# Expert activations of a hybrid scan, attention and mixture kernel: the bias out of the bank first, Gelu in runs of four

## The chip, the cores and the metric

The kernel runs on one core of one Trainium2 chip, in float32. The metric is device time in microseconds (us) of one execution. TensorE multiplies matrices into PSUM banks; VectorE, ScalarE and GpSimd do elementwise work; SyncE (SP) issues nearly all the DMAs. Each engine runs its own queue of instructions strictly in order, and waits on semaphores where an operand comes from another engine.

## The reference, cut to what matters

The input is x of shape (4, 384, 32, 32). Layer 0 is a selective scan in four directions over each image, with 16 states a channel; layer 1 turns the image into 1024 tokens of 384 values per batch, and applies local attention and then a mixture of four experts, of which each token uses two.

```
# layer 0, for each of 4 directions, channel d and state n, over l = 1..1024
dt = softplus(W_dt @ x_dt + bias);  dA = exp(dt * A[d, n])
h[l] = h[l-1] * dA[l] + dt[l] * u[l] * B[n, l];   y[l] += h[l] * C[n, l]
x = x + gelu(layernorm(merge(y)) * lnw + lnb)           # exact gelu
# layer 1
t = t + attention(layernorm(t))                         # 6 heads, causal, window 64
h = gelu(layernorm(t) @ w1[e] + b1[e])                  # 384 -> 1536, exact gelu
t = t + sum over the 2 best experts e of p[e] * (h @ w2[e] + b2[e])
```

Two activation functions matter for what follows. Exp (and Ln) belongs to the decays dA, the time steps dt and the attention's softmax. Gelu belongs to the end of layer 0 and to the experts' first layer.

## The kernel before

**The parts.** Each piece of work is a Python generator. For layer 0: `time_steps` makes dt; `decay` (L830) makes dA = exp(dt * a) on ScalarE, one tile of 128x1024 for each of 768 slots; `times_b` makes z = dt*u*B on GpSimd; `scan` (L856) runs the recurrence on VectorE; `times_c` (L843) multiplies by C, on VectorE or on GpSimd; `fold_y` sums the states with matmuls into a bank ps_y. dA has two buffers of two PSUM banks each (`das_`), so that a decay can only be written when an earlier scan, or the multiplication by C after it, has let go of its buffer. z has seven buffers (`zs_`).

For layer 1: `tokens` (its `tile` is at L986) finishes layer 0 for 128 tokens, with three Gelus on a bank ps_g, and does the attention; `route` picks experts and scatters tokens into rows by expert; `loads` brings in a block of 128 rows and its expert's weights; `hidden` (L1388) is the first layer, `gelus` (L1409) its activation, `output` (L1420) the second layer; `combine` gathers the two results for each token. There are 76 blocks, 19 for each batch. A block's 1536 first-layer values are made in four chunks of 384, each in one PSUM bank ps_hid and then in one tile hs of 128x384, of which there are four. `output` takes a block up when all four of its hs tiles are there.

**What sets the order.** The order of each engine's queue is fixed when the program is built. A planner, `Machine`, keeps a clock per engine and a cost per instruction. Each generator yields its next instruction; `choose` (L338) takes for each engine the one that is ready first, with a bias (`GELU_BIAS`, `LATER` and others). On ScalarE it prefers what needs the activation tables that are loaded now, unless another has been ready for more than 3 us of the planner's time (`PATIENCE`). Where tables change, a table load stands ahead of the activation: the one back to Exp is written by hand (`load_exp_ln`, L304), the one to Gelu has the line of the helper that issues the activation (L148). `Calls` collects several instructions, and `all` (L150) hands them to the planner as one, so that nothing else comes between them. The planner's clocks also decide whether a `times_c` goes to VectorE or GpSimd, and whether copies and some biases go to VectorE or ScalarE. So a change in one place moves instructions everywhere.

**Shared buffers.** Four PSUM banks (`banks`) serve everything but dA: dt, the folds, all the token steps, both expert layers and the routing. When the last scan is done, the two dA buffers join them.

In the profile most instructions have line L148 or L159, the two helpers that issue them, and are told apart by their tiles.

Of the kernel before, what the change touches and what calls it, by code (L numbers as in the profile page):

```python
# [12 lines left out]
AF = mybir.ActivationFunctionType  # L13
# [4 lines left out]
P = 128  # L18
# [18 lines left out]
CH = 384  # L37
NCH, HT = HID // CH, CH // P
# [98 lines left out]
class Engine:  # L137
# [12 lines left out]
    def all(self, calls):  # L150

        asked = [self.ask(*c) for c in calls]
        outs, ins = ([ap for o in asked for ap in getattr(o, side)] for side in ("outs", "ins"))
        table = next((o.table for o in asked if o.table), None)
        whole = Op(self.name, outs, ins, sum(o.cost for o in asked), table, 0)
        whole.work = sum(o.work for o in asked)
        yield whole
        for op, a, k in calls:
            getattr(self.real, op)(*a, **k)  # L159
# [233 lines left out]
def conv_attn_hybrid(  # L393
# [98 lines left out]
    with tc.tile_pool(name="setup", bufs=1) as setup:  # L492
# [16 lines left out]
        for j in range(JB):  # L509
            ps = banks.now("ps_al")  # L510
# [61 lines left out]
    pe, act, dve, pool, sp = m.pe, m.act, m.dve, m.pool, m.sp  # L572
# [315 lines left out]
    ended = []  # L888
# [45 lines left out]
    def three(name, src):  # L934

        yield m.settled(src)
        ps = yield from banks.take(name)
        mm = Calls()
        for t in range(T):
            mm.transpose(ps[:, ts(t, P)], src[:, ts(t, P)], ident)  # L940
        yield from pe.all(mm)
        return ps
# [18 lines left out]
    def normal_of(dst, ps):  # L961
        rn = yield from norm(ps)
        yield from act.activation(dst[:, :D], ps[:, :D], AF.Identity, bias=rn[:, 1:2], scale=rn[:, :1])
        banks.give(ps)
        rns.give(rn)

    def tokens(b):
# [18 lines left out]
        def tile(a):  # L986
# [11 lines left out]
            ps = yield from three("ps_y0", w)  # L998
            yield from normal_of(w, ps)
            g = yield from three("ps_g", w)  # L1000
            for t in range(T):
                yield from act.activation(
                    g[:, ts(t, P)], g[:, ts(t, P)], AF.Gelu,
                    bias=lnb_sb[:, t : t + 1], scale=lnw_sb[:, t : t + 1],
                )
            yield from dve.tensor_tensor(tt[:, :D], g[:, :D], tt[:, :D], ALU.add)
            banks.give(g)
            ps = yield from three("ps_t", tt)
            yield from normal_of(w, ps)
            xt = yield from rows.take("xt")  # L1010
            ps = yield from three("ps_x1", w)
# [7 lines left out]
            for n, (w, dst) in enumerate(  # L1019
                ((wq, q[:, :D].rearrange("p (t l) -> p t l", t=T)), (wk, kv[:, :, :P]))  # L1020
            ):
                ps = yield from banks.take("ps_qk")
                mm = Calls()
# [7 lines left out]
                if not on_vector():  # L1031
                    for o in range(T):
                        yield from act.activation(
                            dst[:, o, :], ps[:, ts(o, P)], AF.Identity,
                            bias=qkb_sb[:, n * T + o : n * T + o + 1],
# [14 lines left out]
            ps = yield from banks.take("ps_v")  # L1050
            mm = Calls()
# [41 lines left out]
            for hp in range(T):  # L1093
                for j in range(2):
                    h = 2 * hp + j
# [29 lines left out]
            mm = Calls()  # L1125
# [22 lines left out]
            ps = yield from three("ps_ot", o)  # L1148
# [3 lines left out]
            ps = yield from banks.take("ps_pr")  # L1152
            on_act = not on_vector()
            mm = Calls()
# [10 lines left out]
            for o in range(T):  # L1165
                c = ts(o, P)
# [12 lines left out]
            ps = yield from three("ps_t2", tt)  # L1179
# [6 lines left out]
            ps = yield from three("ps_xt", tt)  # L1186
            rows.give(tt)
            yield from copy(xt[:, :D], ps[:, :D])
            mm = Calls()
# [8 lines left out]
            have.add(("token", b, a))  # L1198

        yield from m.together([tile(a) for a in range(NT)], TILES, EARLY)  # L1200
        wts.give(wq, wk, wv, wp)

# [156 lines left out]
    rws, bbs, xts, w1s, w2s, hids, left = {}, {}, {}, {}, {}, {}, {}  # L1359
# [28 lines left out]
    def hidden():  # L1388
        for i in range(len(ffn)):
            for c in range(NCH):  # L1390
                hs = yield from hss.take("hs")
                yield lambda: i in xts and (i, c) in w1s
                yield m.settled(xts[i], w1s[i, c])
                ps = yield from banks.take("ps_hid", HID_RANK)
                w = w1s.pop((i, c))
                mm = Calls()
                for j in range(HT):
                    for t in range(T):
                        mm.matmul(
                            ps[:, ts(j, P)], w[:, t * CH + j * P : t * CH + j * P + P],  # L1400
                            xts[i][:, ts(t, P)], start=t == 0, stop=t == T - 1,
                        )
                yield from pe.all(mm)
                wts.give(w)
                if c == NCH - 1:
                    xbts.give(xts.pop(i))
                m.spawn(gelus(i, c, ps, hs), GELU_BIAS)

    def gelus(i, c, ps, hs):  # L1409
        for j in range(HT):  # L1410
            jj = c * HT + j
            yield from act.activation(
                hs[:, ts(j, P)], ps[:, ts(j, P)], AF.Gelu, bias=bbs[i][:, jj : jj + 1]
            )
        banks.give(ps)
        hids[i, c] = hs
        if c == NCH - 1:
            bbs_.give(bbs.pop(i))

    def output():  # L1420
        for i in range(len(ffn)):
            for c in range(NCH):
                yield lambda: (i, c) in hids and (i, c) in w2s
            yield m.settled(*(hids[i, c] for c in range(NCH)))
            y = yield from banks.take("y_ff")
            for c in range(NCH):
                mm = Calls()
                for j in range(HT):
                    mm.matmul(
                        y[:, :D], hids[i, c][:, ts(j, P)], w2s[i, c][:, ts(j, D)],  # L1430
                        start=c == 0 and j == 0, stop=c == NCH - 1 and j == HT - 1,
                    )
                yield from pe.all(mm)
                wts.give(w2s.pop((i, c)))
                hss.give(hids.pop((i, c)))
            m.spawn(leave(i, y), LATER)
# [146 lines left out]
```

## Time and profile before

| | us |
|---|---|
| three runs | 3930.62, 3936.42, 3939.96 (median 3936.42) |
| the profiled execution: its time | 3933.02 |
| its span, first to last instruction | 3931.3 |

| engine | busy us | share of the span | instructions |
|---|---|---|---|
| PE (TensorE) | 3031.9 | 77% | 15880 |
| DVE (VectorE) | 2911.4 | 74% | 3331 |
| POOL (GpSimd) | 2879.7 | 73% | 1498 |
| ACT (ScalarE) | 2441.7 | 62% | 4050 |

The granted TensorE clock has a mean of 0.819 of full speed. DMA moved 953.66 MB, at a mean of 243 GB/s.

A group in the profile reads "line, engine, operation, output tile <- input tiles, shapes, xcount | busy us, mean ns of one | idle us of the engine just before them, and what ended most of it". A wait reads "engine, tile <- the engine and tile that ended the wait: us in total, times, longest us". The largest group of ScalarE is the decay, 768 of 128x1024 at 1116 ns; a scan takes VectorE 2276 to 2287 ns, and times_b takes GpSimd 2358 ns. A line of the timeline is "start us, us, engine, line, operation, xcount", with idle time before it in brackets.

### The profile page before, as it was taken

To read this page: it belongs to the slowest core of one execution; us is meant where nothing else is said; L and a number is where in the kernel's file an instruction comes from. 1 tells how busy PE (TensorE), PEld (TensorE's weight loads), DVE (VectorE), ACT (ScalarE), POOL (GpSimd) and SP (SyncE) were. 2 spreads that over 40 slices of the span, in tenths; PEclk is the share of its full clock that TensorE was granted. 3 is DMA by queue.
4 is the path that set the end of the run, shared out by engine and by line. 5 is a ranking of instruction groups with operands and counts; after the bars stand their busy time and mean duration, and the time that the engine had idled before them with its cause. 6 is when DMAs were issued, how large, how long until landed. Compare 5 with 4: busy or idle time off the path is not lost. (4 is left out here: it accounts for less than half of the span.)

```text
span 3931.3 us, 50281 instructions
## 1 busy us (share of the span) xinstructions
PE 3031.9 (77%) x15880; PEld 1853.6 (47%) x15880; DVE 2911.4 (74%) x3331; ACT 2441.7 (62%) x4050; POOL 2879.7 (73%) x1498
## 2 busy tenths in 40 slices
PE   2555555588677898777687769888878999998997
PEld 1100010055444555434354536556545566877786
DVE  2999999988778788898887797877778884332001
ACT  2544454467787788866667858887677775542221
POOL 1999989988888887898898789888887994012001
PEclk8555566577789899977778879988888999998997
DMA  5776775534558998935377769865567997448995
GB/s 205 266 266 208 275 271 185 193 120 153 175 170 306 329 395 303 336 136 170 107 268 259 259 245 374 293 219 176 182 217 268 363 365 235 143 151 298 318 321 184
DMA packets 394147, 953.66 MB, mean 243 GB/s; under 512 B 49621, under 2 KB 173401, under 8 KB 393881
## 3 DMA queue, kind: packets, MB, share of 16 engines
q1 hardware_dynamic: 385688, 925.27, 67.2%
q0 software_dynamic: 8192, 25.17, 1.8%
q8 instruction: 126, 2.06, 0.2%
q14 instruction: 141, 1.15, 0.1%
HBM read 786.39 MB, written 182.78 MB: 247 GB/s over the span
## 5 line engine op out<-in xcount | busy, mean ns | idle before, releaser
L148 POOL TENSOR_TENSOR z<-dts,bc 128x1024 f32<-128x1024 f32 x768 | 1793.4, 2358 | 178.5 <-PE ps_y L159 93.6
L148 ACT ACTIVATE dA<-dts,a 128x1024 f32<-128x1024 f32 x768 | 851.7, 1116 | 473.7 <-DVE z L148 448.8
L159 PE MATMUL ps_y<-z,fold 128*32 128x512 f32 x3072 | 730.6, 771 | 487.7 <-POOL z L148 262.9
L148 POOL TENSOR_TENSOR z<-z,bc 128x1024 f32<-128x1024 f32 x383 | 898.2, 2356 | 139.7 <-DVE z L148 130.0
L148 DVE TENSOR_TENSOR_SCAN dA<-dA,z 128x1024 f32<-128x1024 f32 x385 | 880.6, 2287 | 135.5 <-ACT dA L148 128.5
L148 DVE TENSOR_TENSOR_SCAN z<-dA,z 128x1024 f32<-128x1024 f32 x383 | 862.3, 2276 | 57.0 <-ACT dA L148 54.5
L159 PEld LDWEIGHTS ps_hid<-xbt,w_sb 128*128 128x128 f32 x5472 | 674.4, 200 | 152.8 <-issue 50.7
L159 PE MATMUL ps_hid<-xbt,w_sb 128*128 128x128 f32 x5472 | 698.9, 286 | 48.8 <-DMA w_sb<-wl 13.1
L159 PE MATMUL y_ff<-w_sb,hs 128*128 128x384 f32 x1824 | 659.7, 503 | 28.8 <-ACT hs L148 17.8
L159 PEld LDWEIGHTS ps_y<-z,fold 128*32 128x32 f32 x3072 | 93.8, 120 | 915.3 <-POOL z L148 448.2
L148 DVE TENSOR_TENSOR z<-dA,bc 128x1024 f32<-128x1024 f32 x385 | 470.0, 1221 | 13.2 <-DVE dA L148 0.5
L148 ACT ACTIVATE hs<-ps_hid,bb 128x128 f32<-128x128 f32 x912 | 276.2, 368 | 306.3 <-PE ps_hid L159 255.4
L159 PEld LDWEIGHTS y_ff<-w_sb,hs 128*128 128x128 f32 x1824 | 333.7, 195 | 276.1 <-issue 58.4
L148 POOL DMA_INDIRECT cb<-ysdr,idx x64 | 62.6, 978 | 320.0 <-DMA ysdr<-yb 274.1
L148 ACT ACT_TABLE_LOAD x194 | 248.9, 1283 | 10.3 <-PE ps_g L159 3.6
L304 ACT ACT_TABLE_LOAD x194 | 248.9, 1283 | 4.1 <-PEq L1568 0.8
L159 POOL TENSOR_TENSOR rn<-rn,half 128x1 f32<-128x1 f32 x96 | 52.8, 550 | 212.2 <-DVE rn L159 203.2
L148 DVE COPY yb<-y_ff 128x384 f32<-128x384 f32 x24 | 13.4, 557 | 248.8 <-PE y_ff L159 233.3
L148 ACT ACTIVATE ed<-ps_dt,dtb_sb 128x512 f32<-128x512 f32 x192 | 125.4, 681 | 83.9 <-PE ps_dt L148 78.8
L148 POOL DMA_INDIRECT xsdr<-tks,idx x64 | 65.1, 1016 | 141.8 <-DVE idx L159 56.6
L148 PE MATMUL ps_dt<-xd,dtw_sb 12*128 12x512 f32 x192 | 135.6, 816 | 20.0 <-DMA dtw_sb<-in_dtw_dram 14.7
L148 DVE TENSOR_TENSOR ps_dt<-ps_dt,ed 128x512 f32<-128x512 f32 x192 | 132.7, 691 | 11.7 <-ACT ps_dt L148 8.8
(202 smaller groups left out, 3293.8 us busy)
## 6 DMA issues: line engine op xcount, KB each, us to landing
w_sb<-wl SPq DMA_DIRECT2D x608, 576.0 KB
dts<-dtr SPq DMA_DIRECT2D x384, 512.0 KB
bc<-xdr SPq DMA_DIRECT2D x128, 512.0 KB
dtr<-ed SPq DMA_DIRECT2D x192, 256.0 KB
ub<-udr SPq DMA_DIRECT2D x48, 512.0 KB
yp<-ydr SPq DMA_DIRECT2D x96, 256.0 KB
ydr<-yp SPq DMA_DIRECT2D x96, 256.0 KB
wl<-in_w_dram SPq DMA_DIRECT2D x32, 576.0 KB
```

The lines of the kernel that those rows point to most:

```text
L148: return getattr(self.real, op)(*a, **k)
L159: getattr(self.real, op)(*a, **k)
L304: self.nc.scalar.add_instruction(mybir.InstLoadActFuncSet(name=self.nc.get_next_instruction_name(), act_func_set_id=EXP_LN_SET,))
```

## The change

There are two edits. The first is in `tile` of `tokens`: the three Gelus on ps_g, which were three separate steps of the planner, become one run.

The second is in `gelus`. As long as scans remain (`ended` is still empty when the chunk's activation begins), a chunk of first-layer values leaves its bank with Identity and the bias, in three instructions as before, and the bank is given back. When all four chunks of the block have left their banks, one run of four Gelus follows, each over a whole hs tile of 128x384 in place and without a bias. Only then are the four tiles handed to `output`. Once the scans are over, the bias and Gelu are one activation out of the bank, as before; the handing over in fours remains.

```
             g = yield from three("ps_g", w)
+            mm = Calls()
             for t in range(T):
-                yield from act.activation(
+                mm.activation(
                     g[:, ts(t, P)], g[:, ts(t, P)], AF.Gelu,
                     bias=lnb_sb[:, t : t + 1], scale=lnw_sb[:, t : t + 1],
                 )
+            yield from act.all(mm)
...
     def gelus(i, c, ps, hs):
+        late = not ended
+        f = AF.Identity if late else AF.Gelu
         for j in range(HT):
             jj = c * HT + j
             yield from act.activation(
-                hs[:, ts(j, P)], ps[:, ts(j, P)], AF.Gelu, bias=bbs[i][:, jj : jj + 1]
+                hs[:, ts(j, P)], ps[:, ts(j, P)], f, bias=bbs[i][:, jj : jj + 1]
             )
         banks.give(ps)
-        hids[i, c] = hs
-        if c == NCH - 1:
+        plain[i, c] = hs
+        if late:
+            unbent.setdefault(i, []).append(hs)
+        if all((i, n) in plain for n in range(NCH)):
             bbs_.give(bbs.pop(i))
+            mm = Calls()
+            for h in unbent.pop(i, ()):
+                mm.activation(h[:, :CH], h[:, :CH], AF.Gelu)
+            if mm:
+                yield from act.all(mm)
+            for n in range(NCH):
+                hids[i, n] = plain.pop((i, n))
+
+    plain, unbent = {}, {}
```

## The prediction, made before the result

> **What bounds the kernel now.** I read the busy time by stage first, because the page's average mixes two stages. The last decay-and-scan pair stands at 3276 us, so I cut at 3280. Columns: us, then busy us and (instructions) of PE, PEld, DVE, ACT, POOL, then granted PE clock, DMA share, GB/s.
>
> ```profile
> 0.00:3280.00 3280.00, 2425.80 (x12090) 1359.86 (x12091) 2778.74 (x2846) 2237.71 (x3457) 2814.01 (x1402) 0.79 0.69 244
> 3280.00:3932.00 652.00, 606.15 (x3793) 493.71 (x3791) 132.68 (x485) 204.00 (x593) 65.65 (x97) 0.94 0.70 234
> ```
>
> While scans run, VectorE (85%) and GpSimd (86%) are nearly full; ScalarE has 68%. Afterwards TensorE is the bound (606 of 652 us, 93%). So ScalarE is no bound by its busy time. It counts only where it makes VectorE late. Second, then, who waited for whom in the first stage (engine, tile, releaser: us, times, longest), and the groups (busy us, mean ns | idle before):
>
> ```profile
> DVE dA L148 <- ACT dA L148: 128.5, 67, 5.4
> DVE z L148 <- ACT dA L148: 54.5, 40, 4.3
> POOL z L148 <- DVE z L148: 130.0, 65, 8.8
> POOL z L148 <- PE ps_y L159: 93.6, 54, 6.5
> ...
> L148 POOL TENSOR_TENSOR z<-z,bc 128x1024 f32<-128x1024 f32 x383 | 898.2, 2356 | 139.7 <-DVE z L148 130.0
> L148 DVE TENSOR_TENSOR z<-dA,bc 128x1024 f32<-128x1024 f32 x385 | 470.0, 1221 | 13.2 <-DVE dA L148 0.5
> L148 ACT ACTIVATE hs<-ps_hid,bb 128x128 f32<-128x128 f32 x912 | 276.2, 368 | 306.3 <-PE ps_hid L159 255.4
> L148 ACT ACT_TABLE_LOAD x194 | 248.9, 1283 | 10.3 <-PE ps_g L159 3.6
> L304 ACT ACT_TABLE_LOAD x194 | 248.9, 1283 | 4.1 <-PEq L1568 0.8
> ```
>
> The first two lines are the sum to remember: a scan waited for its decay, dA, 107 times, 182.9 us in all. Third, ScalarE's timeline at such a wait (start us, us, operation):
>
> ```profile
> 2711.94 1.28 ACT L148 ACT_TABLE_LOAD   x1
> 2713.24 0.37 ACT L148 ACTIVATE hs<-ps_hid,bb 128x128 f32<-128x128 f32 x1
> 2713.62 1.28 ACT L304 ACT_TABLE_LOAD   x1
> 2714.92 1.12 ACT L148 ACTIVATE dA<-dts,a 128x1024 f32<-128x1024 f32 x1
> ...
> 2716.14 2.30 DVE L148 TENSOR_TENSOR_SCAN dA<-dA,z 128x1024 f32<-128x1024 f32 x1 [1.07 <-ACT dA L148]
> ```
>
> One Gelu of 0.37 us costs 2.57 us of loads, and the scan behind it is 1.07 us late. Over the whole trace I counted the waits for dA with a table load on ScalarE in the 4 us before: 88 of 107, with 165.3 of the 182.9 us.
>
> **What the Trainium skill says.** "ScalarE: Activation LUTs", section "What ACT_TABLE_LOAD costs", gives 1283 ns for a load and a drain of 1380 ns more. The trace agrees on the load (1283) and not on the drain: above, the Gelu starts 0.02 us after its load, so I count 1.28 us a load. The same page, "Table sets: the hidden batching unit", says that cheap functions such as identity are in every set. The trace agrees: copies stand between Gelus (v at 2705.56, in the Gelu set) with no load around them. So the new Identity needs no switch. "GPSIMD Engine Reference", section "Engine selection", has two-input work about 2x slower on GpSimd than on VectorE; here 2356 against 1221 ns.
>
> **The change part by part.** Counts of the changed kernel come from comparing the order of instructions in the two built programs, which holds no times.
>
> *Loads.* 388 table loads become 160: 228 x 1.283 = 292.5 us less on ScalarE. Both kinds of Gelu share in it: those of the expert layer (50 runs of four while scans run) and those of the tokens (three in one run).
>
> *Identity for Gelu out of the bank.* Same instruction count, 912. q and k leave their bank by Identity with a bias at the same shape in 365 ns; Gelu takes 368. Nothing.
>
> *The added Gelus.* 200 of 128x384, SBUF to SBUF, no bias. No such row is in the trace. The nearest, Exp from SBUF to SBUF at 128x512, takes 625 ns; less 128 x 0.833 ns (ScalarE: Activation LUTs, its rate per element) it is 518. Three hs acts of 0.37 take 0.88 together, so neighbours overlap by 0.11. A run is 4 x 0.518 - 3 x 0.11 = 1.74 us; 50 runs are 87 us. ScalarE: 87 - 292 = -205 us. By itself this is worth nothing.
>
> *VectorE's waits for decays.* Of the 768 stretches between decays on ScalarE, 176 hold a switch before and 69 after. Before, one costs VectorE 165.3/176 = 0.94 us. After, one lasts longer: a run with its loads is 1.28 + 1.74 + 1.28 = 4.30 us; the commonest stretch in Gelu's tables before was one hs act (58 of 193), 2.93 us. That is 1.37 us more. If the two dA buffers cover the extra, the waits fall to 69 x 0.94 = 65 us (saves 100); if they cover none, to 69 x 2.31 = 159 us (saves 6). I take the middle, 53. VectorE's other waits for ScalarE in this stage are 100.8 us, 34.4 of them within 4 us of a load; I take 10 (0 to 20). What is late next is the scan's own z from GpSimd and the fold that frees z.
>
> *Work that moves.* The planner, which picks the engine of each times_c by its own clocks, gives 24 more to VectorE: 24 x 1.221 = 29.3 us, and some small copies and adds, 2 us. GpSimd loses 24 x 2.356 = 56.5 us.
>
> *The bank comes free early.* ps_hid is given back after three Identities, with no wait for Gelu's tables. All of TensorE's users share four banks, and VectorE waits for TensorE in some ten rows of this stage (48.1 us for ps_y the longest). No row prices it: 0 to 30 us, I take 10.
>
> *The wait that is added.* A block's activations reach the second layer only when all four chunks are bent. Its loop waited for all four before, so this costs nothing there; the four hs tiles are held as before. What is queued behind the run on ScalarE is the next decay, the softmax exponentials and the time steps; VectorE waits for the first, which is the 1.37 us above. No DMA is added or moved past another; SP and GpSimd get no new wait.
>
> *First stage.* VectorE: -53 - 10 - 10 + 31 = -42 us. GpSimd: -56 if it gains no idle time; it waits for VectorE (130 us of its idle), so it follows. Ends: -100 - 20 - 30 + 31 = -119, and -6 + 31 = +25.
>
> *Second stage.* After the last fold TensorE has 927 first-layer and 321 second-layer matmuls, before 891 and 309: one more block. In busy time a block is (698.9 + 659.7)/76 = 17.9 us, and this stage has almost no room: +18 us (0 if it fills TensorE's 46 idle us).
>
> Sum: -42 + 18 = -24 us. The profiled execution took 3933.0 (span 3931.3, 1.7 outside it), so 3909. It lies 3.4 us below the median of 3936.4; against the median I forecast 3936.4 - 24 = 3912.
>
> **Rivals.** *A, the forecast*: 3912, own range 3890 to 3928. For it: nine tenths of the waits follow a load, and the loads fall by 59%; against it: the middle of 6 to 100 is a choice.
> *B, the runs are wholly covered and the bank helps*: -100 - 20 - 10 + 31 = -99 and +18: 3855, with 3835 to 3890 around it. For it: the decays run ahead by a second buffer (ScalarE waits 448.8 us for VectorE to free one). Against: that second buffer is what already left 0.94 us a stretch uncovered.
> *C, the saving goes into another wait*: the scan finds its decay, but not its z. GpSimd waits 130.0 us for VectorE and 93.6 for folds, and VectorE has 31 us more to do. Within 8 us of 3936.
> *D, slower: one long run in front of the decay.* Place: the decay right behind the four Gelus. Price: only 6 us of waits saved, none of the small items, 31 us of work moved to VectorE, 18 us of tail: 3936 - 6 + 31 + 18 = 3979; I put the case at 3962, with the small items. It decides once a stretch with a switch costs VectorE more than (165.3 - 29)/69 = 1.98 us: 29 is what A's sum needs from these waits to break even (31 + 18 - 10 - 10). For it: 1.98 lies well below the 2.31 of no cover.
> *E, the loads stay*, because Identity would want tables of its own. The built program has 160 loads, so I give it nothing.
>
> **How the numbers follow.** A 0.45, B 0.12, C 0.18, D 0.25. About 0.2% (8 us) is what a measurement of this kernel can tell from no change. Faster: nearly all of A, and B: 0.55. Same: C and a little of A: 0.20. Slower: D, 0.25. The range leaves out half of B and somewhat under half of D: 3860 to 3962. It is wide because the cover of a run is bounded by 6 and 100 us only.
>
> **What would show it.** Right: 160 loads in two groups of 80; a new group hs<-hs near 518 ns; scans' waits for dA, with the 17.6 us that no load explains, between 83 and 177 us, near 130; the last scan some 40 us earlier than 3276; the tail some 18 us longer. Wrong: waits for dA above 69 x 1.98 + 17.6 = 154 us and the last scan not earlier (D); waits down but GpSimd's idle time for VectorE or the folds up by as much (C); a tail that changes by far more than one block, because the order of the last tokens and blocks was laid out anew, which no term here covers.

## The result, and the profile after

The changed kernel takes 3882.0 us (median of four runs, 3878.9 to 3884.0), the kernel before on the same chip 3938.2. The ratio is 0.9855, with a 95% interval of 0.984 to 0.9871: 1.45% or 57 us faster. The forecast was 24 us faster. The sign held, the size did not. The profiled execution after took 3882.5 us (span 3880.8).

First the busy time by stage, cut at the end of the last scan, which is now at 3204.2 us and was at 3278.7.

```profile
0.00:3204.20 3204.20, 2404.88 (x11972) 1331.87 (x11973) 2805.94 (x2869) 2017.60 (x3416) 2757.72 (x1377) 0.80 0.70 248
3204.20:3880.80 676.60, 628.48 (x3897) 509.87 (x3897) 134.73 (x489) 209.16 (x602) 66.67 (x97) 0.94 0.70 233
```

The first stage is 74.5 us shorter, and the second 24.0 us longer (652.6 before, cut the same way): together -50.5 us, the difference of the two spans. In the first stage ScalarE's busy time falls from 2237 to 2018 us, but VectorE's rises from 2778.7 to 2805.9. So VectorE's gain lies in its idle time, 500.0 us before and 398.2 now. Who ended its waits, and GpSimd's:

```profile
DVE dA L148 <- ACT dA L148: 77.7, 61, 5.2
...
DVE z L148 <- ACT dA L148: 28.6, 24, 3.6
```
```profile
POOL z L148 <- PE ps_y L159: 105.8, 50, 5.4
POOL z L148 <- DVE z L148: 96.2, 52, 6.2
```

The scans' waits for decays, 128.5 + 54.5 us before, are now 77.7 + 28.6. The groups of the page, and then those of ScalarE from the list that keeps shapes apart:

```profile
L148 POOL TENSOR_TENSOR z<-z,bc 128x1024 f32<-128x1024 f32 x359 | 841.7, 2355 | 110.8 <-DVE z L148 96.2
L148 DVE TENSOR_TENSOR z<-dA,bc 128x1024 f32<-128x1024 f32 x409 | 499.1, 1220 | 13.8 <-DVE dA L148 0.5
```
```profile
L304 ACT ACT_TABLE_LOAD x80 | 102.6, 1283 | 2.2 <-PEq L1583 0.8
L159 ACT ACT_TABLE_LOAD x71 | 91.1, 1283 | 7.2 <-PE ps_g L159 6.2
L159 ACT ACTIVATE hs<-hs 128x384 f32<-128x384 f32 x200 | 88.2, 511 | 0.6
...
L148 ACT ACT_TABLE_LOAD x9 | 11.5, 1283 | 0.2
```

80 loads each way, as counted; a Gelu of a whole hs tile takes 511 ns (518 was forecast), and four in a row 1.76 us (1.74). The unit prices were right. What such a run looks like where it costs nothing, first ScalarE and then VectorE (start us, us, operation):

```profile
2377.98 2.14 ACT L148 ACTIVATE dA<-dts,a 128x1024 f32<-128x1024 f32 x2
...
2381.97 1.28 ACT L159 ACT_TABLE_LOAD   x1
2383.27 1.76 ACT L159 ACTIVATE hs<-hs 128x384 f32<-128x384 f32 x4
2384.94 0.56 ACT L148 COPY ed<-ps_dt 128x512 f32<-128x512 f32 x1
2385.52 1.28 ACT L304 ACT_TABLE_LOAD   x1
2386.82 1.12 ACT L148 ACTIVATE dA<-dts,a 128x1024 f32<-128x1024 f32 x1
```
```profile
2379.76 2.29 DVE L148 TENSOR_TENSOR_SCAN dA<-dA,z 128x1024 f32<-128x1024 f32 x1
...
2385.53 2.28 DVE L148 TENSOR_TENSOR_SCAN dA<-dA,z 128x1024 f32<-128x1024 f32 x1
...
2388.99 2.28 DVE L148 TENSOR_TENSOR_SCAN z<-dA,z 128x1024 f32<-128x1024 f32 x1
```

Two decays stand just ahead of the run. VectorE uses the first at 2379.76 and the second at 2385.53, and the third is done at 2387.94, a microsecond before VectorE gets to it. Over the whole trace, 49 stretches between decays hold such a run; they last 6.33 us on average and cost the scan behind them 1.16 us. Before, 155 stretches with Gelus of the experts and none of the tokens lasted 5.40 us and cost 0.97 us each.

Where do these stretches grow? From the start of their first load to the end of their last they take 4.84 us before and 4.86 now, so the long run keeps ScalarE no longer than what it replaced. What has grown is the time from the last decay to the first load, 0.5 us before and 1.5 now: other work that stands ahead of the run. VectorE's supply has grown as much there: at the end of the last decay VectorE was 4.6 us on average from the end of the scan that uses this decay, and is 5.5 now. At the first load it is 4.1 before and 4.0 now.

### The profile page after: what moved, and what is told of

Read it like the earlier page. It is cut to its first block, busy times and chain, and to the rows that moved or that the text cites. A ratio compares the mean times of both kernels' runs of the same rounds, so it can differ in the third digit from the quotient of the medians.

```text
span 3880.8 us, 50273 instructions
## 1 busy us (share of the span) xinstructions
PE 3033.4 (78%) x15868; PEld 1841.7 (47%) x15868; DVE 2940.7 (76%) x3358; ACT 2226.8 (57%) x4017; POOL 2824.4 (73%) x1474
## 5 line engine op out<-in xcount | busy, mean ns | idle before, releaser
L148 DVE TENSOR_TENSOR_SCAN dA<-dA,z 128x1024 f32<-128x1024 f32 x409 | 935.6, 2288 | 93.2 <-ACT dA L148 77.7
L148 POOL TENSOR_TENSOR z<-z,bc 128x1024 f32<-128x1024 f32 x359 | 841.7, 2355 | 110.8 <-DVE z L148 96.2
L148 DVE TENSOR_TENSOR_SCAN z<-dA,z 128x1024 f32<-128x1024 f32 x359 | 807.8, 2276 | 31.6 <-ACT dA L148 28.6
L159 PE MATMUL y_ff<-w_sb,hs 128*128 128x384 f32 x1824 | 680.8, 515 | 58.5 <-ACT hs L159 46.4
L148 DVE TENSOR_TENSOR z<-dA,bc 128x1024 f32<-128x1024 f32 x409 | 499.1, 1220 | 13.8 <-DVE dA L148 0.5
L148 ACT COPY ed<-ps_dt 128x512 f32<-128x512 f32 x96 | 56.0, 584 | 124.8 <-DVE ed L148 124.5
L304 ACT ACT_TABLE_LOAD x80 | 102.6, 1283 | 2.2 <-PEq L1583 0.8
```

The costliest lines, as they stand in the source:

```text
L148: return getattr(self.real, op)(*a, **k)
L304: self.nc.scalar.add_instruction(mybir.InstLoadActFuncSet(name=self.nc.get_next_instruction_name(), act_func_set_id=EXP_LN_SET,))
```

## The experiments

Two things changed at once: the loads went, and the planner, which knows what a load costs, laid out every queue anew. The theory 'loads' has the gain come from the first, 'layout' from the second, and 'banks' from the bank that comes free earlier. Times are given as ratios to the kernel before measured in the same batch, and in us worked out from them at 3938 us (1% is 39 us). Figures of idle time come from each kernel's profiled execution, VectorE's up to the end of the last scan; "near a load" is within 4 us of one on ScalarE.

| kernel | loads | ratio, 95% interval | last scan ends, us | waits for decays near a load | other waits for decays | waits for TensorE |
|---|---|---|---|---|---|---|
| before | 388 | 1 | 3278.7 | 165.3 | 17.6 | 149.2 |
| the change | 160 | 0.9855 (0.984 to 0.9871) | 3204.2 | 69.1 | 37.5 | 108.6 |
| e1 tokens only | 378 | 0.9955 (0.9937 to 0.9973) | 3279.5 | 121.4 | 20.7 | 149.1 |
| e2 experts only | 168 | 0.9869 (0.9852 to 0.9887) | 3212.5 | 104.1 | 47.9 | 109.2 |
| e3 Gelu by chunk | 348 | 1.0001 (0.9989 to 1.0013) | 3297.1 | 149.8 | 33.9 | 132.4 |
| e4 three from the bank | 360 | 0.9962 (0.995 to 0.9974) | 3258.2 | 92.7 | 22.9 | 150.3 |
| e5 loads back | 388 | 1.0389 (1.0365 to 1.0413) | 3406.0 | 215.2 | 27.9 | 124.2 |
| e6 before, no loads | 1 | 0.9789 (0.9765 to 0.9813) | 3211.7 | 0 | 70.1 | 191.5 |
| e7 the change, no loads | 1 | 0.9759 (0.9726 to 0.9791) | 3189.5 | 0 | 59.5 | 136.1 |
| e8 split pinned | 160 | 0.9896 (0.9871 to 0.9921) | 3237.0 | 82.3 | 30.5 | 135.0 |
| e9 long runs | 260 | 1.0125 (1.0097 to 1.0152) | 3312.5 | 158.9 | 48.5 | 110.7 |
| e10 loads behind decays | 388 | 1.0094 (1.0058 to 1.0129) | 3291.8 | 117.0 | 24.8 | 123.9 |
| p3 before, LEAD 0.7 | 390 | 1.0176 (1.0151 to 1.0201) | 3313.2 | 145.4 | 19.9 | 152.1 |
| p4 the change, LEAD 0.7 | 156 | 0.9885 (0.9854 to 0.9916) | 3194.1 | 64.0 | 41.7 | 133.5 |
| p5 p3, no loads | 1 | 0.9991 (0.9982 to 1.0001) | 3233.0 | 0 | 66.2 | 184.2 |
| p6 p4, no loads | 1 | 0.9802 (0.9786 to 0.9818) | 3163.5 | 0 | 61.8 | 155.9 |
| v1 PATIENCE 6 | 160 | 0.988 (0.9863 to 0.9896) | 3233.1 | 77.6 | 51.8 | 112.7 |

**The parts of the change.** e1 takes only the first edit, e2 only the second; their diffs are the two halves of the diff above.

> Only the tokens' three Gelus become one run; the experts' part is as before. The program has 378 table loads (before 388, the change 160). Theory 'loads' (the gain is in proportion to the loads that vanish from in front of decays: 56 us for 228): 10 loads are worth 2 us, so about 3936. Theory 'layout' (any change makes the planner lay all queues out anew, and the gain is a lucky layout): may be anywhere between 3880 and 3990.

> Only the experts' part of the change: Identity out of the bank and runs of four Gelus. 168 loads. Theory 'loads': 220 of 228 loads go, about 3884. Theory 'layout': no number, but there would be no reason to land near 3882.

e1 gained 0.45%, 18 us, where 'loads' had 2. Its last scan ends where it did before; its gain lies after it, where TensorE has one and a quarter blocks less to do (846 first-layer matmuls against 891), which at 17.9 us a block is 22 us. In the profiled executions that stage lasts 640.6 us against 652.6. That is layout, and a miss of 'loads'. e2 gained 1.31%, 52 us, close to the 54 that 'loads' had. The experts' part carries the change.

e3 keeps the early bank and drops the batching by block; e4 drops both, and issues the three Gelus of a chunk, out of the bank, as one run. The cuts are against the changed kernel.

```
 # e3, in gelus
         banks.give(ps)
-        plain[i, c] = hs
+        if late:
+            yield from act.activation(hs[:, :CH], hs[:, :CH], AF.Gelu)
+        hids[i, c] = hs
...
 # e4, in gelus
+        mm = Calls()
         for j in range(HT):
             jj = c * HT + j
-            yield from act.activation(
-                hs[:, ts(j, P)], ps[:, ts(j, P)], f, bias=bbs[i][:, jj : jj + 1]
+            mm.activation(
+                hs[:, ts(j, P)], ps[:, ts(j, P)], AF.Gelu, bias=bbs[i][:, jj : jj + 1]
             )
+        yield from act.all(mm)
         banks.give(ps)
...      # from here on as before the change
```

> The change, but each chunk gets its own Gelu of 128x384 right after its three Identities, so the bank comes free early, and the batching by block is gone. 348 loads, 163 stretches between decays that hold a switch (before 388 and 176; the change 160 and 69). Theory 'loads': 40 of 228 loads, about 10 us, 3928. Theory 'banks' (the early release of the bank makes the gain, through VectorE's waits for TensorE, which fell by 41 us): keeps most of the gain, 3890 to 3900.

> Gelu straight out of the bank as before, but the three of a chunk in one run that nothing can split; the tokens' run as in the change. 360 loads, 166 stretches with a switch; the bank is held until Gelu's tables are there. Theory 'loads': 28 of 228 loads, 7 us, 3931. Theory 'banks': no gain or a loss, 3935 to 3950, since the bank now waits for the tables in one piece.

e3 gained nothing (1.0001), where 'loads' had 10 us and 'banks' most of the gain. An early bank alone is not enough to make the kernel fast. VectorE's waits for TensorE are lower there (132 us against 149), but ScalarE has 207 more Gelus to do and still 348 loads. e4 is 0.38% or 15 us faster with the bank held as long as before: with the three Gelus of a chunk in one piece, 166 stretches with a switch cost 93 us of scans' waits, where 176 cost 165. Each of e1 to e4 is one plan, and the pairs of plans at the end of this section differ by 12 and by 74 us with no loads in them; so these four alone don't decide between the theories.

**The loads out of a fixed order.** In e6 and e7 each Gelu is issued as Identity, while the planner still takes it for a Gelu; the kernel then leaves Gelu out. No load is left but the first, and the other instructions keep their order on every engine.

```
         yield self.ask(op, a, k)
-        return getattr(self.real, op)(*a, **k)
+        return getattr(self.real, op)(*plainly(a), **k)   # AF.Gelu becomes AF.Identity
...
             if op.table == "exp_ln":
-                self.load_exp_ln()
+                pass
```

> The kernel before with no table load after the first: every Gelu is issued as Identity (Gelu is left out of the computation), in exactly the order of before on every engine. Theory 'loads': VectorE's 165 us of waits for decays near a load and 34 us of its other waits near one go; if nothing takes their place 3938 - 199 = 3739, if half of it is taken over by other waits 3840. Theories 'banks' and 'layout': the order is unchanged, so only the bank's shorter hold is gained, 3890 to 3930.

> The changed kernel with no table load after the first: every Gelu is issued as Identity (Gelu is left out of the computation), in exactly the changed kernel's order. Theory 'loads': 69 us of waits for decays near a load and 18 us of others go, so 3795 to 3840, and the difference to the kernel before without loads is small (within 15 us), since that leaves only layout, moved work and banks between the two. Theory 'layout': the two differ by the 56 us that the change is worth.

Without its 387 later loads the kernel before is 2.11% or 83 us faster; without its 159 the changed one is 0.96% or 38 us faster. So of the 57 us the loads make 45 (with an uncertainty of about 17, from the three intervals), and all the rest, which is the new plan, the moved work, the added Gelus and the earlier bank, about 12 (0.9789 against 0.9759, whose intervals overlap: on its own not clear of nothing). 'Loads' is the main cause at this setting. It had the two kernels without loads within 15 us of each other, which held. But it was far off on the size for e6, where I had expected 98 to 199 us (the other theories 8 to 48), and somewhat off for e7 (42 to 87). The reason stands in the waits of the kernel before, over its whole run, and in e6's:

```profile
DVE yp L148 <- PE ps_y L159: 51.9, 36, 4.8
...
DVE o L148 <- PE ps_o L159: 39.4, 21, 4.0
```
```profile
DVE yp L152 <- PE ps_y L163: 72.0, 45, 6.5
DVE dA L152 <- ACT dA L152: 51.8, 36, 4.7
...
DVE o L152 <- PE ps_o L163: 42.2, 22, 4.0
```

The waits for decays near a load are gone, 165.3 us; but other waits for decays rise from 18 to 70 us, and waits for TensorE from 149 to 192 (for the fold, ps_y, from 51.9 to 72.0 over the whole run). Some 95 us of the 165 were only what hid another wait. VectorE's other waits for ScalarE hardly change in sum (101 us before, 94 in e6): those near a load go, others rise. A load taken out of the plan that was made with it saves 83/387 = 0.21 us in the kernel before and 38/159 = 0.24 in the changed one, a sixth of its 1.28 us.

**The loads put back into a fixed order.** e5 and e10 put back 228 idle loads (Exp's tables over Exp's) in two places, e9 lengthens each run by two loads. In the traces the other instructions of all three stand in the changed kernel's order on every engine.

```
 # e5, in gelus behind the second and third Identity
+            if late and j > 0 and m.table == "exp_ln" and len(extra) < 228:
+                extra.append(i)
+                m.load_exp_ln()
...
 # e10, in decay behind every second decay
+            if s >= 270 and s % 2 == 0 and len(extra) < 228:
+                extra.append(s)
+                m.load_exp_ln()
...
 # e9, in gelus: a load of Exp's tables between the second and third Gelu of a run
             if mm:
+                mm.insert(2, ("add_instruction", None, None))
                 yield from act.all(mm)
```

> The changed kernel with 228 idle table loads (Exp's tables over Exp's tables) put back, one behind the second and third Identity of a chunk while scans run: 388 loads in all, as many as before. All other instructions stand in exactly the changed kernel's order on every engine. 147 stretches between decays then hold two loads or more, instead of 69. Theory 'loads': 78 more such stretches at the 1.00 us that one costs now, +78, about 3960; at least the whole gain is lost. Theories 'banks' and 'layout': the order and the banks are the change's, ScalarE has room, so within 15 us of 3882.

> The changed kernel with 228 idle loads put back, but one right behind every second decay from slot 270 on, where VectorE's stock of decays is fullest; the order of everything else is the changed kernel's. 388 loads. Theory 'place' (what a load costs depends on how many decays lie ready, and on who waits behind it): well below the 215 us that the same 228 loads cost behind Identities, 40 to 110 us. Theory 'any unplanned load costs alike': again about 215 us, 4097.

> The changed kernel with two more table loads in the middle of each of the 50 runs of four Gelus (to Exp's tables and back), 260 loads in all, in the same 69 stretches between decays; every other instruction stands in the changed kernel's order on every engine. Each run is 2.57 us longer. This measures the disputed term, what of a longer run VectorE's two dA buffers cover. Half covered, as the prediction took: 50 x 1.28 = +64 us, 3946. Four fifths covered, as the trace after suggests (its stretches with a run are 0.93 us longer than those of before and cost 0.19 us more each): 50 x 0.5 = +26 us, 3908. At the 0.94 us a load that the idle loads behind Identities cost: +94, 3976.

Against the changed kernel e5 costs 5.34%, 210 us or 0.92 a load; e10 2.39%, 94 us or 0.41 a load; e9 2.70%, 106 us or 1.06 for each of its 100 added loads. 'Banks' and 'layout' had e5 within 15 us, and are out for what these loads cost; 'place' held for e10; but each cost more than 'loads' had for e5 (78) and than any figure I had for e9 (26 to 94). A run of e9, and its waits:

```profile
1156.21 1.28 ACT L160 ACT_TABLE_LOAD   x1
1157.51 0.94 ACT L160 ACTIVATE hs<-hs 128x384 f32<-128x384 f32 x2
1158.46 1.28 ACT L307 ACT_TABLE_LOAD   x1
1159.75 1.28 ACT L160 ACT_TABLE_LOAD   x1
1161.05 0.94 ACT L160 ACTIVATE hs<-hs 128x384 f32<-128x384 f32 x2
1162.00 1.28 ACT L307 ACT_TABLE_LOAD   x1
1163.29 1.12 ACT L148 ACTIVATE dA<-dts,a 128x1024 f32<-128x1024 f32 x1
```
```profile
DVE dA L148 <- ACT dA L148: 154.5, 67, 7.2
DVE z L148 <- ACT dA L148: 52.7, 35, 5.3
```

The run, from its first load to the decay, is 7.08 us long. The scans' waits near a load rise from 69.1 to 158.9 us, 90 us for 50 runs: of 2.57 us more, 1.8 are not covered. So the two dA buffers covered only some 30% of what was added. VectorE's supply at the first load is the changed kernel's (4.1 us against 4.0), and it does not reach that far. ScalarE's free time in the stage as a whole is of no help there.

Why an added load costs more than one taken out saves is not shown. The planner may place better what it knows of, or the first loads may use up the slack and later ones find none. In e3 the planner itself placed 188 loads more than in the changed kernel, and e3 is 57 us slower, 0.31 us a load, less than in e5, e9 and e10. That speaks for the planner, but it compares two plans.

**The moved work, and other plans.** e8 fixes the engine of each multiplication by C to the choice of before.

```
-            on_pool = count_of["times"] >= min(s + AHEAD, NSLOT) and m.clock["pool"] < m.clock["dve"] + LEAD
+            on_pool = PINNED[s] == "1"
```

> The changed kernel, with the engine of each multiplication by C fixed to the choice of before (383 on GpSimd, 385 on VectorE, slot by slot), so that the 24 that moved to VectorE are back. 160 loads, 70 stretches with a switch. Theory 'loads': waits as in the change; VectorE has 29 us less and GpSimd 56 us more to do, which about cancels, 3875 to 3905. Theory 'layout' in its form that the new split between the two engines makes the gain: back to 3925 or more.

It keeps 1.04% of the 1.45%: 41 us of 57. The new split, with the order that comes with it, is worth some 16 us, with an uncertainty of about 12: with the old split VectorE has less to do (2766 us against 2806) but waits more (470.6 us idle against 398.2). Its median of 3901.8 lies at the upper end of what 'loads' had (3875 to 3905), and well below the 3925 of the other theory.

p3 and p4 are the two kernels at LEAD = 0.7 instead of 0.6, p5 and p6 the same without loads, and v1 is the change with PATIENCE = 6.0.

> The kernel before with another setting of the planner: LEAD, its lean toward GpSimd for the multiplication by C, 0.7 instead of 0.6. 390 loads, other queues on every engine, 369 multiplications on GpSimd (before 383), one and three quarter blocks more left for the time after the scans than before. Theory 'loads': as before but for the layout. Theory 'layout' (plans scatter by tens of us): far from 3941, by 20 us or more either way.

> The changed kernel with LEAD 0.7: 156 loads. With the kernel before at the same setting it repeats the change under other plans. Theory 'loads': below that one by 45 to 60 us again. Theory 'layout': the difference of the two is something else, it may vanish or turn.

> The kernel before at LEAD 0.7, its order on every engine unchanged, with no table load after the first: every Gelu is issued as Identity (Gelu is left out of the computation). Theory 'loads': 389 loads cost 0.22 us each as in the plan of before (83 us for 387), so 4013 - 85 = 3928. If the 121 us that the change gains at this setting are mostly the loads' doing in a plan less able to hide them, more: 100 to 140 us, near 3890.

> The changed kernel at LEAD 0.7, its order unchanged, with no table load after the first: every Gelu is issued as Identity (Gelu is left out). Theory 'loads': 155 loads at 0.24 us, 3892 - 37 = 3855. Its difference to the kernel before at LEAD 0.7 without loads is what the plans alone differ by at this setting: within 15 us by theory 'loads', most of 121 us by theory 'layout'.

> The changed kernel with PATIENCE 6 instead of 3: an activation that needs the other tables waits up to 6 us of the planner's time. It still has 160 loads and 69 stretches with a switch, but one and a half blocks fewer after the last scan (873 first-layer matmuls against 927). Theory 'loads': the loads are the same, so 3882, less at most 27 us (1.5 blocks of 17.9 us) if the scans end no later: 3855 to 3890. Theory 'layout': anywhere within 50 us of 3882.

A constant changed by 0.1 makes the kernel before 1.76% slower, 69 us, more than the whole change is worth; at that setting the change gains 2.91% of the first kernel's time, 115 us (121 between the medians). 'Loads' had 45 to 60 us for this, a miss. Without loads the two gain 1.85% and 0.83%: the loads' share is 1.02%, 40 us, as at 0.6 (45), again with an uncertainty of about 17. The other 1.89%, 74 us, is plan. So at these two settings the loads' share repeats and the plan's does not: 12 us at one, 74 at the other, where the plan is the larger part. 'Loads' had p5 and p6 right (3936.3 us against 3928, 3859.9 against 3855), but not the difference of p5 and p6, 76 us between the medians where it had at most 15; 'layout' had most of 121. The traces of p5 and p6 show where their difference lies: in p5 VectorE has 27 us more work before the last scan (2815.4 against 2788.1), waits 42 us longer, 28 of them for TensorE, and the time after the scans is 8 us longer. Why the planner lays the queues so stays open. v1 has as many loads as the change and is 0.25% or 10 us slower than it (the intervals overlap a little), and just above what 'loads' had (3891 us against 3855 to 3890), though it leaves one and a half blocks less for the end: its last scan is 29 us later. No version beat the change among those that compute the same.

## Why the prediction was right in sign and wrong in size

In profiled executions the forecast was -42 us for the first stage and +18 for the second; measured were -74.5 and +24.0. By VectorE's account of the first stage:

| term | forecast, us | measured, us |
|---|---|---|
| scans' waits for decays | -53 | -76.3 (182.9 to 106.6) |
| other waits for ScalarE | -10 | +8.5 (100.8 to 109.3) |
| waits for TensorE ("the bank comes free early") | -10 | -40.6 (149.2 to 108.6) |
| VectorE's work | +31 | +27.2 |
| waits for GpSimd and DMA | 0 | +7.9 |
| sum | -42 | -73.3, of -74.5 |
| second stage | +18 | +24.0 |

**Waits for decays: mis-sized, because the time in Gelu's tables did not grow.** The step made it 1.37 us longer than before, had the two dA buffers cover between all and none of that, and took half: 1.62 us a stretch. Measured are 69.1/69 = 1.00 us, against 0.94 before. What failed first is the 1.37 us. It sets the run of four, 4.30 us, against one hs act, 2.93 us, which the text calls the commonest, 58 of 193. Of these 58, 31 hold one act and 27 hold three, which the timeline prints as one line, x3. On average a stretch took 4.84 us from its first load to the end of its last before, and takes 4.86 now. With nothing added the step's own sum gives 65 us of waits, 100 saved; measured are 69, 96 saved. The choice of the middle does not explain the miss: in e9, where the run really is 2.57 us longer, 70% of that reaches the scans. Of the gain, 20 us was lost again in waits for decays with no load near (17.6 to 37.5), a term that I had held constant.

**The bank: mis-sized by 31 us, and its reason not shown.** The term had no price and got 10. The waits for TensorE did fall by 41. But e3, which frees the bank as early, has them at 132 us against 149, and e6, where the bank waits for no tables, has more of them (192 us). Few switches do not settle it either: plans with 156 to 168 loads have 109 us (e2), 113 (v1), 134 (p4) and 135 (e8). What made these waits fall stays open.

**Other waits for ScalarE: wrong in sign.** They rose; those near a load fell from 34 to 18 us, and others took their place.

**Moved work and the tail: right.** 24 multiplications moved, at 1220 ns, against GpSimd's 2355. The tail gained the one block that the order showed: TensorE's busy time there rose from 607.5 to 628.5 us, 21 against 17.9, the rest is idle time.

**The rivals.** B came nearest to the measured time, 27 us off against 30 for A, and in part by luck: a stretch costs hardly more than before, as B had it, but because it keeps ScalarE in Gelu's tables no longer, and not because the buffers cover more. C was not how it ended, but its mechanism is real: e6 shows that more than half of what loads cost the scans comes back as other waits. In the changed kernel GpSimd's waits for VectorE fell (130.0 to 96.2 us), and those for folds rose by 12. D's mechanism is real as well, and its price too: in e9 a stretch with a switch costs 158.9/69 = 2.30 us, above D's point of 1.98, and the kernel is slower than before. It did not come to pass because a run of the change, with its loads, is no longer than what it replaced. What the prediction lacked was a term for the plan as a whole: it costed each moved instruction, and took the rest of the plan to be as good as before.

## What to carry to other kernels

Where the queues are laid out by a planner, price a removal in three parts: the instruction itself in the fixed order, what takes its place there, and the new plan. The first two together came out alike at two settings (45 and 40 us, each with some 17 of uncertainty); the third scattered by as much as the change is worth, so judge an edit at two settings of the planner before trusting its size. When one long piece of work replaces many short ones, compare it with the mean of what it replaces, and not with the commonest case. And time that an engine has to spare is not time at the place where an edit puts its work: on a ScalarE that was busy for 63% of its stage, a load of 1.28 us added to a finished plan cost up to 1.06 us, and one taken out saved 0.2.

## What the runs showed of the hardware that was not expected

A table load is not skipped when the tables are there already: e5's idle loads take as long as any, 1283 ns.

```profile
L304 ACT ACT_TABLE_LOAD x308 | 395.2, 1283 | 4.9 <-PEq L1586 0.8
```

Of these 308, 228 load Exp's tables over Exp's. And in e9 two loads in a row, at 1158.46 and 1159.75, start 1.29 us apart, so that a load needs no more than its own length even behind another.
